# A four-layer network on one core: one lane of layer 1 at a time, an output product moved, and another start for the first head pair

## The chip, the core and the metric

The kernel runs on one core of one Trainium2 chip. The core has a matrix engine (PE, with its weight loads shown as PEld), a vector engine (DVE), a scalar engine (ACT), a general engine (POOL), and a sync engine (SP) that mostly issues transfers (DMA). They run side by side and wait for one another through semaphores. The metric is the device time of one execution in microseconds (us), lower is better. The kernel before takes 3713.06 us (median of 3 runs, 3712.05 to 3713.46).

## The reference

The input is `x`, 4 samples of 256 channels on a 48 x 48 grid (2304 positions), in float32. Four residual layers follow one another, each on the group-normalised `x`. Cut to what matters:

```python
x = x + L0(gn(x))   # 8 heads of 64: q, k, v = w_qkv @ x; q, k normalised over the positions;
                    # softmax(10 * q.k) over 2304 positions; times v; w_out
x = x + L1(gn(x))   # 3x3 max pool, blur to 16x16, depthwise taps along four directions,
                    # gate = sigmoid(sum), upsampled by 3; gn(x) * gate
x = x + L2(gn(x))   # one-head attention, softmax(theta.phi / 8), W, batch norm over all samples
x = x + L3(gn(x))   # channel gate, 3x3 depthwise convolution, instance norm, leaky relu

def _gn(v, G=32, eps=1e-5):
    g = v.reshape(B_, G, C_ // G, H_, W_)
    m, s = g.mean((2, 3, 4)), g.var((2, 3, 4))
    return (g - m) / sqrt(s + eps)
```

Layer 0 is by far the largest: 4 samples x 8 heads x 2304 x 2304 scores.

## The kernel before

Channels lie on 128 partitions in two halves (`k` = 0, 1). Layer 0 works sample by sample and head pair by head pair: 16 phases (4 samples `b` x 4 pairs `p`). A phase has 6 units of 384 query columns; a unit has 9 groups of 256 keys. Layer 2's attention follows with 12 more units, so there are 108. The main loop issues, for each group `t`, the scores of this group, the sums of the softmax denominators of the group before, work that is due in this place, and then the product with v of the group before. Beside it run "lanes": generators that issue a few instructions of other layers between the groups.

```python
for t, (u, g, st) in enumerate(groups):
    for j in range(g * G, (g + 1) * G):
        scores(u, j)                       # PE, then exp on ACT
    if prev is not None:
        add_up(*prev)                      # POOL (half), DVE (acc)
    do(due, t)
    ...
    do(fills, t)                           # jobs of this place, in the order of their rank
    clock["early"] = False
    lanes(st["others"], st, t + 0.5, ends) # other layers
    ...                                    # then weigh(pu, j): the product with v
    if pg == NG - 1:
        last(pu, t)                        # ACT copies av to raw; ends a unit
```

In the third group of a unit (`AT_CHUNK` = 2) stands the projection of the next pair, in the order of the ranks: q (1), v (2), then the output product of an earlier unit, half 0 (2.5), then k (3), then half 1 (4). All of them take turns in two PSUM tiles `pj`.

```python
def chunk(s):
    def end():
        qk(s, 1)
        squares(s)
        if s + 2 < NCH:
            fetch(s + 2)                   # 384 columns of x from memory into a tile xs
    return [(1, lambda: qk(s, 0)), (2, lambda: values(s)), (3, end)]

def out_proj(b, p, c, pair, o):
    ...
    return [((2.5, 4)[k], lambda k=k: part(k)) for k in range(NK)]
```

Layer 1 of sample b runs beside layer 0 of sample b + 1. For samples 0 to 2 it is one generator for both halves: statistics, maxima, blur, then 20 "rounds" of tap products (ACT) and sums (DVE), then the gate, its products with x (POOL) and additions (DVE). The places in a unit in which it may go on are given by `TURNS`, and by `ROUND` or `HASTE` for the rounds:

```python
TURNS, ROUND, HASTE = (2, 2, 3, 5, 6, 8), -1, -2
ROUND_TURNS = {ROUND: (2, 5, 8), HASTE: (2, 4, 6, 8)}
...
haste = HASTE if b == NX - 1 else ROUND    # NX = 3
...
for i, (b, p) in enumerate(order):
    ...
    if (b, p) == (2, 0):
        for s in range(NSL):
            work.setdefault(s + 2 * NG, []).append(lambda s=s: send(s))      # sample 0 to memory
            work.setdefault(s + 5 * NG, []).append(lambda s=s: receive(s))   # sample 3 in its place
    if b > 0:
        end = n - 2 if (b, p) == (B - 1, NPAIR - 1) else n + 1
        others.append((l1[b - 1], FREE, 2 if p == 0 else 0, end))
    if b > 1 and p == 0:
        others.append((l1[b - 2], FREE, 0, 4 * NG))
```

In the place `end - 1` of a phase a lane is run to its end at once, whatever is left of it. With `n + 1` this place never comes.

The start: x of sample 0 is loaded, group statistics are taken, and the first pair is projected from fetched tiles of x, chunk by chunk, before the attention begins:

```python
projs[0]["prefetch"]()                     # weights of pair 0
_drain(gn(0, norms0[0]))
projs[0]["norms"]()                        # weights times 1/deviation (ACT), bias for v
projs[0]["start"]()                        # fetches the first two tiles of x again
projs[1]["prefetch"]()
for s in range(NCH):
    for _, fn in projs[0]["chunk"](s):     # q, v, k, squares of q and k
        fn()
for fn in projs[0]["scale"]:               # 1/norms, q scaled
    fn()
projs[0]["out_bias"]()
projs[1]["norms"]()
for b in range(1, NX):
    load_x(b)                              # samples 1 and 2
attend(phases)
```

Of the kernel before, what the change touches and what calls it, by code (L numbers as in the profile page):

```python
# [14 lines left out]
P = 128  # L15
HW = 48
N = HW * HW
NK = 2
# [56 lines left out]
def usual_path(  # L75
# [27 lines left out]

    def load_x(b):
        for k in range(NK):
            nc.sync.dma_start(X[b][:, k, :], xv[:, k, b, :])

    load_x(0)
    vec = cpool.tile([P, 9, NK], F32, name="vec")
    nc.scalar.dma_start(vec, vecs)  # L110

# [34 lines left out]
    )  # L146
    ones = cpool.tile([P, D], F32, name="ones")
    nc.gpsimd.memset(ones, 1.0)
    mhalf = cpool.tile([P, NK], F32, name="mhalf")
    nc.gpsimd.memset(mhalf, -0.5)  # L150
    nb1 = cpool.tile([P, NK], F32, name="nb1")
    nc.vector.tensor_scalar(nb1, vec[:, V_B1, :], -1.0, None, ALU.mult)

# [10 lines left out]

    GN_TICKS = NSL + 4

    def gn(b, res, halves=range(NK), slices=range(NSL)):

        if "st" not in res:
            res["st"] = small.tile([P, NK, NSL, 6], F32, tag="gn_st", name="gn_st")  # L170
        st = res["st"]
        for s in slices:
            for k in halves:
                nc.vector.bn_stats(st[:, k, s, :], X[b][:, k, s * SL : (s + 1) * SL])
            if s % 2 or len(halves) == NK:
                yield 0
        mv = small.tile([P, NK, 2], F32, tag="gn_mv", name="gn_mv")
        for k in range(NK):
            nc.vector.bn_aggr(mv[:, k, :], st[:, k].rearrange("p s f -> p (s f)"))
        yield 3  # L180
        ps = pj_tile()
        nc.tensor.matmul(ps[:, 0:NK], lhsT=gmat, rhs=mv[:, :, 0], start=True, stop=True)
        gm = small.tile([P, NK], F32, tag="gn_gm", name="gn_gm")
        nc.vector.tensor_copy(gm, ps[:, 0:NK])
# [200 lines left out]
    def attend(phases):  # L385


        groups = []
        for units, work, others in phases:
            for slot, fns in work.items():  # L390
                fills.setdefault(len(groups) + slot, []).extend(fns)
            st = {"others": [[gen, n, a, z, 0, 0] for gen, n, a, z in others], "at": 0}
            groups += [(u, g, st) for u in units for g in range(NG)]
        prev = None

        def lanes(some, st, t, ends):
            for lane in some:
                gen, n, a, z, done, ready = lane
                until = -(-n * (st["at"] + 1 - a) // (z - a))
                clock["final"] = final = st["at"] == z - 1  # L400
                while final or (done < until and t >= ready and not ends):
                    wait = next(gen, None)
                    if wait is None:
                        break
                    done, ready = done + 1, t + wait
                lane[4:] = done, ready

        def do(table, t):

            jobs = [job if isinstance(job, tuple) else (5, job) for job in table.pop(t, ())]  # L410
            for _, fn in sorted(jobs, key=lambda job: job[0]):
                fn()

        for t, (u, g, st) in enumerate(groups):
            for j in range(g * G, (g + 1) * G):
                scores(u, j)
            if prev is not None:
                add_up(*prev)
            do(due, t)

            ends = prev is not None and prev[1] == NG - 1
            clock["t"], clock["slot"] = t, st["at"] % NG

            clock["early"] = True
            if clock["slot"] == AT_AFTER % NG:
                lanes([lane for lane in st["others"] if lane[1] == FREE], st, t, ends)
            do(fills, t)
            clock["early"] = False
            lanes(st["others"], st, t + 0.5, ends)
            st["at"] += 1  # L430
            if prev is not None:
                pu, pg = prev
                for j in range(pg * G, (pg + 1) * G):
                    weigh(pu, j)
                if pg == NG - 1:
                    last(pu, t)
            prev = (u, g)
        pu, pg = prev
        add_up(pu, pg)
        for j in range(pg * G, (pg + 1) * G):  # L440
            weigh(pu, j)
        last(pu, len(groups))
        for t in sorted(set(due) | set(fills)):
            do(fills, t)
            do(due, t)
# [3 lines left out]
    def project(b, norm, pair):  # L449

        p = pair["p"]
        xs = {}
        at = {}

# [28 lines left out]
        def start():  # L483
            pair["q"] = big.tile([P, N], F32, tag="q", name="q")
            pair["k"] = big.tile([P, N], F32, tag="k", name="k")
            pair["v"] = big.tile([P, JB, P], F32, tag="v", name="v")
            at["ss"] = small.tile([P, 2, NSL], F32, tag="ss", name="ss")
            at["bias"] = small.tile([P, 2], F32, tag="bias", name="bias")
            fetch(0)
            fetch(1)  # L490

        def out_bias():
            ps = pj_tile()
# [12 lines left out]
        def qk(s, t):  # L506
            cols = slice(s * SL, (s + 1) * SL)
            to = pair["qk"[t]][:, cols]
            n = SL + (s == 0)
            ps = pj_tile()  # L510
            for k in range(NK):
                nc.tensor.matmul(  # L512
                    ps[:, :n], lhsT=at["w"][:, k, t, :], rhs=xs[s][:, k, :n],
                    start=k == 0, stop=k == NK - 1,
                )
            if s == 0:
                nc.scalar.copy(at["bias"][:, t : t + 1], ps[:, SL:n])
            nc.scalar.activation(to, ps[:, :SL], AF.Identity, bias=at["bias"][:, t : t + 1])  # L518

        def squares(s):  # L520

# [38 lines left out]
        def rescale(c0, c1):  # L560
# [8 lines left out]

        return {  # L570
            "prefetch": prefetch, "norms": norms, "start": start, "out_bias": out_bias,
            "chunk": chunk,
            "scale": [
                scale, lambda: rescale(0, 1), lambda: rescale(1, 3), lambda: rescale(3, 6)
            ],
# [2 lines left out]
    def out_proj(b, p, c, pair, o):  # L578
# [11 lines left out]
                xs, ps[:, :SL], pair["bo"][:, k : k + 1], xs, ALU.add, ALU.add  # L590
            )

        return [((2.5, 4)[k], lambda k=k: part(k)) for k in range(NK)]

    def l0_unit(b, p, c, pair):
        hold = {}
# [68 lines left out]
    ]  # L665
    L1_BUF = (NT + 1) * AS * AS

    TURNS, ROUND, HASTE = (2, 2, 3, 5, 6, 8), -1, -2
    ROUND_TURNS = {ROUND: (2, 5, 8), HASTE: (2, 4, 6, 8)}

    def paced(gen):

        at, count, wait, turns = -9, 0, 0, TURNS
        while True:
# [9 lines left out]
            if wait is None:  # L684
                return
            at, count = t, count + 1
            turns = ROUND_TURNS.get(wait, TURNS)
            yield 0

    def maxima(b, k, res):  # L690
# [60 lines left out]

    def strips(b, k, norm, res):


        haste = HASTE if b == NX - 1 else ROUND
        pd = padded(k, norm, res)

        bufs = [
# [11 lines left out]
                )  # L770

        products(0)
        yield haste
        products(1)
        yield haste
        for n, taps in enumerate(ROUNDS):
            last = n == len(ROUNDS) - 1
            if n + 2 < len(ROUNDS):
# [5 lines left out]
            nc.vector.tensor_reduce(  # L784
                to, bufs[n % 3][:, :, : min(n, 1) + len(taps)], AX.X, ALU.add
            )
            yield haste

    TAPS_AT_ONCE = 12

# [370 lines left out]
    for i, (b, p) in enumerate(order):  # L1161
# [16 lines left out]
                work[NG * s + AT_CHUNK] = slices[s]  # L1178
        if (b, p) == (2, 0):
            for s in range(NSL):  # L1180
                work.setdefault(s + 2 * NG, []).append(lambda s=s: send(s))
                work.setdefault(s + 5 * NG, []).append(lambda s=s: receive(s))
        if (b, p) == (0, 0):
            others.append((tap_weights(), WEIGHT_TICKS, 2, n - 2))
        if b > 0:
            end = n - 2 if (b, p) == (B - 1, NPAIR - 1) else n + 1
            others.append((l1[b - 1], FREE, 2 if p == 0 else 0, end))
        if b > 1 and p == 0:
            others.append((l1[b - 2], FREE, 0, 4 * NG))
        if (b, p) == (B - 1, NPAIR - 1):  # L1190
            others.append((part(ahead, L1_AHEAD, False), L1_AHEAD, n - L1_AHEAD - 3, n))
        if p == 1 and b + 1 < B:
# [30 lines left out]
        phases.append(([l2_unit(b, c, twos[b]) for c in range(L2C)], work, others))  # L1223

    projs[0]["prefetch"]()
    _drain(gn(0, norms0[0]))
    projs[0]["norms"]()
    projs[0]["start"]()
    projs[1]["prefetch"]()
    for s in range(NCH):  # L1230
        for _, fn in projs[0]["chunk"](s):
            fn()
    for fn in projs[0]["scale"]:
        fn()
    projs[0]["out_bias"]()
    projs[1]["norms"]()
    for b in range(1, NX):
        load_x(b)
    attend(phases)
    for k in range(NK):  # L1240
        w_stats(B - 1, k, L2C - 1)
# [1214 lines left out]
```

## Time and profile before

| | before |
|---|---|
| median of the runs | 3713.06 us |
| span of the profiled run | 3710.8 us |
| mean granted clock of PE | 0.980 |
| first scores of layer 0 | 51.9 us |
| layer 0, all samples, beside layer 1 of samples 0 to 2 | 51.9 to 2992 us |
| layer 2's attention, beside layer 1 of sample 3 | 2992 to 3442.8 us |
| layer 3 | 3442.8 us to the end |
| DMA | 97.89 MB, mean 26 GB/s |

The costliest rows of the profile are these. The columns are: line, engine, operation, output and input tiles, shape, count; then busy time in us and the mean of one in ns; then the idle time of the engine just before them and what ended it.

```profile
L244 ACT ACTIVATE pt<-sc 128x768 f32<-128x768 f32 x1944 | 1476.5, 812 | 814.1 <-PE sc L238 805.4
L269 POOL TENSOR_TENSOR half<-pt 128x768 f32<-128x768 f32 x477 | 954.1, 2001 | 1673.4 <-ACT pt L244 1611.7
L238 PE MATMUL sc<-q,k 64*64 64x384 f32 x13824 | 1279.6, 485 | 12.7 <-ACT pt L244 9.9
L258 PE MATMUL av<-pt,v 64*64 64x384 f32 x13824 | 1279.8, 485 | 0.0
L284 DVE TENSOR_TENSOR acc<-acc,pt 128x768 f32<-128x768 f32 x792 | 930.7, 1175 | 86.2 <-DVE acc L284 1.8
```

PE waits for almost nothing before its two large groups of matmuls, while ACT and POOL wait much for PE and ACT. A busy PE in such a table means that instructions follow one another without a gap; a matmul's end is modelled, so start to start is the better measure of one.

### The profile page before, as it was taken

The numbers are of one execution on the slowest core, as the hardware profiler recorded it, in microseconds if no ns is written. First come the engines' busy times: TensorE is split into PE (matmuls) and PEld (weight loads), VectorE is DVE, ScalarE is ACT, GpSimd is POOL, SyncE is SP. The second block draws the span as 40 slices with busy tenths as digits, with TensorE's granted clock in tenths as the row PEclk, the third lists the DMA queues.
The fourth block names the chain that finished last, engine by engine and source line by source line (L and its number), as shares of the span: only waits on it lengthen the run. The fifth ranks groups of instructions, "written<-read, shape, count | busy, mean of one in ns | idle before, by whom it ended". The sixth has DMA issues, their size and how long they took to land.

```text
span 3710.8 us, 86538 instructions
## 1 busy us (share of the span) xinstructions
PE 3522.4 (95%) x36330; PEld 1759.4 (47%) x36330; DVE 2588.3 (70%) x3203; ACT 2344.5 (63%) x3819; POOL 1444.7 (39%) x900
## 2 busy tenths in 40 slices
PE   7999999999999999999999999999999998999685
PEld 4444444454444444444444444444444445654343
DVE  2455555476778777967787779767968786576687
ACT  4665666666776677557766775587578555555353
POOL 2333333333334333433343334433433455664242
PEclk9999999999999999999999999999999999999797
DMA  4111111111111111121111111111111100000001
GB/s 138 24 25 21 26 21 26 21 25 21 25 21 26 20 29 17 34 55 34 21 25 21 25 21 25 21 25 21 25 16 25 17 6 6 6 8 4 26 29 74
DMA packets 114591, 97.89 MB, mean 26 GB/s; under 512 B 56224, under 2 KB 111632, under 8 KB 112400
## 3 DMA queue, kind: packets, MB, share of 16 engines
q1 hardware_dynamic: 111728, 91.27, 12.8%
q8 instruction: 286, 4.69, 0.5%
q10 hardware_dynamic: 2464, 1.00, 0.1%
q14 instruction: 113, 0.93, 0.1%
HBM read 59.33 MB, written 11.80 MB: 19 GB/s over the span
## 4 chain that ended last, share of the span: by engine, by line
PE 68%; DVE 18%; issue 5%; ACT 4%; POOL 3%; DMA 2%; SPq 0%; DVEq 0%; ACTq 0%; POOLq 0%
PE av L258 26%; PE sc L238 26%; DVE acc L284 7%; PE pj L512 6%; PE pj L584 3%; PE pj L533 3%; DVE sc L1446 2%; PE pj L291 1%; POOL half L269 1%; ACT pt L244 1%; DVE av L1446 1%; DVE acc L278 1%; PE pj L828 1%; ACT prod L766 1%; DMA xs<-in_x_dram 1%
## 5 line engine op out<-in xcount | busy, mean ns | idle before, releaser
L244 ACT ACTIVATE pt<-sc 128x768 f32<-128x768 f32 x1944 | 1476.5, 812 | 814.1 <-PE sc L238 805.4
L269 POOL TENSOR_TENSOR half<-pt 128x768 f32<-128x768 f32 x477 | 954.1, 2001 | 1673.4 <-ACT pt L244 1611.7
L238 PE MATMUL sc<-q,k 64*64 64x384 f32 x13824 | 1279.6, 485 | 12.7 <-ACT pt L244 9.9
L258 PE MATMUL av<-pt,v 64*64 64x384 f32 x13824 | 1279.8, 485 | 0.0
L284 DVE TENSOR_TENSOR acc<-acc,pt 128x768 f32<-128x768 f32 x792 | 930.7, 1175 | 86.2 <-DVE acc L284 1.8
L238 PEld LDWEIGHTS sc<-q,k 64*64 64x64 f32 x13824 | 510.6, 133 | 638.2 <-issue 499.9
L258 PEld LDWEIGHTS av<-pt,v 64*64 64x64 f32 x13824 | 514.4, 133 | 594.0 <-issue 557.3
L284 DVE TENSOR_TENSOR acc<-acc,half 128x768 f32<-128x768 f32 x459 | 468.6, 1021 | 335.7 <-POOL half L269 334.1
L589 DVE SCALAR_TENSOR_TENSOR x<-pj,bo,x 128x384 f32<-128x384 f32 x192 | 118.0, 615 | 461.9 <-PE pj L584 461.7
L512 PE MATMUL pj<-xs,w 128*128 128x384 f32 (+1 forms) x768 | 298.5, 512 | 3.2 <-issue 1.7
L766 ACT ACTIVATE prod<-pd,wt 128x256 f32<-128x256 f32 x486 | 280.6, 743 | 0.2
L339 POOL TENSOR_TENSOR o<-o,rinv 128x384 f32<-128x384 f32 x95 | 128.9, 1356 | 284.3 <-DMA rinv<-rinv 273.2
L512 PEld LDWEIGHTS pj<-xs,w 128*128 128x128 f32 x768 | 131.0, 190 | 157.3 <-issue 53.9
L584 PE MATMUL pj<-o,wo 128*128 128x384 f32 x384 | 159.8, 501 | 33.3 <-DVE x L589 28.7
L258 PE MATMUL av<-pt,qv 64*64 64x384 f32 x1728 | 173.9, 496 | 0.0
L238 PE MATMUL sc<-qv,kd 64*64 64x384 f32 x1728 | 169.4, 486 | 2.4 <-ACT pt L244 2.4
L784 DVE TENSOR_REDUCE prod<-prod 128x256 f32<-128x1280 f32 x114 | 168.5, 1478 | 0.0
L278 DVE TENSOR_TENSOR acc<-pt 128x768 f32<-128x768 f32 x99 | 139.3, 1407 | 26.4 <-ACT pt L244 26.4
L533 PEld LDWEIGHTS pj<-w,xs 128*128 128x128 f32 x1152 | 143.8, 192 | 26.0 <-issue 0.6
L533 PE MATMUL pj<-w,xs 128*128 128x128 f32 x1152 | 144.1, 275 | 0.0
L518 ACT ACTIVATE k<-pj,bias 128x384 f32<-128x384 f32 x96 | 55.7, 580 | 127.5 <-PE pj L512 127.0
L335 POOL TENSOR_TENSOR o<-raw 128x384 f32<-128x384 f32 x95 | 117.7, 1238 | 0.0
(226 smaller groups left out, 2686.7 us busy)
## 6 DMA issues: line engine op xcount, KB each, us to landing
xs<-in_x_dram SPq DMA_DIRECT2D x96, 384.0 KB
rinv<-rinv SPq DMA_DIRECT2D x208, 94.5 KB
x<-in_x_dram SPq DMA_DIRECT2D x6, 1152.0 KB
out_dram<-x SPq DMA_DIRECT2D x6, 1152.0 KB
l<-row SPq DMA_DIRECT2D x416, 1.5 KB
w<-in_wqkv_dram SPq DMA_DIRECT2D x32, 192.0 KB
rinv<-ls SPq DMA_DIRECT2D x208, 1.5 KB
x_out<-x SPq DMA_DIRECT2D x6, 384.0 KB
```

The source lines that it names most:

```text
L238: nc.tensor.matmul(ps[c * D : (c + 1) * D, h, :SL], lhsT=u["of"]["k"][r, j0 : j0 + D], rhs=u["of"]["q"][r, u["qc"]], start=True, stop=True,)
L244: nc.scalar.activation(pt, ps[:, :, :SL], AF.Exp, scale=u["scale"])
L258: nc.tensor.matmul(u["av"][h * D : (h + 1) * D, half, :SL], lhsT=value(u, j, h)[r], rhs=pt[r, h, :], start=j == 0, stop=j == JB - 1,)
L269: nc.gpsimd.tensor_add(half, pts[0], pts[1])
L278: nc.vector.tensor_add(u["acc"], ready[0], ready[1])
L284: nc.vector.tensor_add(u["acc"], u["acc"], term)
L339: eng.tensor_mul(o, o, u["rinv"])
L512: nc.tensor.matmul(ps[:, :n], lhsT=at["w"][:, k, t, :], rhs=xs[s][:, k, :n], start=k == 0, stop=k == NK - 1,)
L533: nc.tensor.matmul(ps[:, i * P : (i + 1) * P], lhsT=xs[s][:, k, i * P : (i + 1) * P], rhs=at["w"][:, k, 2, :], start=k == 0, stop=k == NK - 1,
L584: nc.tensor.matmul(ps[:, :SL], lhsT=wo[:, p, k * P : (k + 1) * P], rhs=o["o"], start=True, stop=True,)
L766: nc.scalar.activation(bufs[n % 3][:, :, min(n, 1) + i].rearrange("p (r c) -> p r c", c=AS), pd[:, PAD + dr : PAD + dr + AS, PAD + dc : PA ...
L784: nc.vector.tensor_reduce(to, bufs[n % 3][:, :, : min(n, 1) + len(taps)], AX.X, ALU.add)
```

## The change

It has three parts. Layer 1 of a sample must end within the four pairs of the next sample, so that there is never more than one lane of it, and its rounds go at the quicker pace for all three samples; sample 0 is then complete when sample 2 begins, and its store and the load of sample 3 move to the front of that sample. In sample 0's phases the first half of the output product comes directly after the scores, ahead of the sums and of the projections, so that the two PSUM tiles are taken in another order. At the start, x of sample 0 comes in over two queues, the statistics are taken half by half, the ACT table is loaded ahead, and the first pair is projected from x itself with q and k of all chunks ahead of v; DVE empties the k tiles; x of samples 1 and 2 is loaded later.

```diff
     def load_x(b):
         for k in range(NK):
-            nc.sync.dma_start(X[b][:, k, :], xv[:, k, b, :])
+            eng = nc.scalar if b == 0 and k else nc.sync
+            eng.dma_start(X[b][:, k, :], xv[:, k, b, :])
...
+    warm = cpool.tile([P, 1], F32, name="warm")
+    nc.scalar.activation(warm, mhalf[:, 0:1], AF.Exp)
...
+        if first:                              # group statistics of sample 0
+            for k in halves:
+                for s in slices:
+                    nc.vector.bn_stats(st[:, k, s, :], X[b][:, k, s * SL : (s + 1) * SL])
...
             for j in range(g * G, (g + 1) * G):
                 scores(u, j)
+
+            do(fills, t, lambda rank: rank < 1)
             if prev is not None:
                 add_up(*prev)
...
+            if direct:                         # start() of the first pair
+                for s in range(NSL):
+                    xs[s] = X[b][:, :, s * SL : (s + 1) * SL]
+            else:
+                fetch(0)
+                fetch(1)
...
+            if s == 0 and direct:              # qk(): the mean as a column of its own
+                for k in range(NK):
+                    nc.tensor.matmul(
+                        ps[:, SL : SL + 1], lhsT=at["w"][:, k, t, :],
+                        rhs=norm["nm"][:, k : k + 1], start=k == 0, stop=k == NK - 1,
+                    )
             if s == 0:
-                nc.scalar.copy(at["bias"][:, t : t + 1], ps[:, SL:n])
-            nc.scalar.activation(to, ps[:, :SL], AF.Identity, bias=at["bias"][:, t : t + 1])
+                nc.scalar.copy(at["bias"][:, t : t + 1], ps[:, SL : SL + 1])
+            if direct and t:
+
+                nc.vector.tensor_scalar(to, ps[:, :SL], at["bias"][:, t : t + 1], None, ALU.add)
+            else:
+                nc.scalar.activation(to, ps[:, :SL], AF.Identity, bias=at["bias"][:, t : t + 1])
...
-        return [((2.5, 4)[k], lambda k=k: part(k)) for k in range(NK)]
+        return [((2.5 if b else 0, 4)[k], lambda k=k: part(k)) for k in range(NK)]
...
-    TURNS, ROUND, HASTE = (2, 2, 3, 5, 6, 8), -1, -2
-    ROUND_TURNS = {ROUND: (2, 5, 8), HASTE: (2, 4, 6, 8)}
+    TURNS, ROUND, ROUND_TURNS = (2, 2, 3, 5, 6, 8), -1, (2, 4, 6, 8)
...
         if (b, p) == (2, 0):
             for s in range(NSL):
-                work.setdefault(s + 2 * NG, []).append(lambda s=s: send(s))
-                work.setdefault(s + 5 * NG, []).append(lambda s=s: receive(s))
+                work.setdefault(s, []).append(lambda s=s: send(s))
+                work.setdefault(s + NG, []).append(lambda s=s: receive(s))
         if (b, p) == (0, 0):
+            for c in range(1, NX):
+                work.setdefault(10 * c, []).append(lambda c=c: load_x(c))
             others.append((tap_weights(), WEIGHT_TICKS, 2, n - 2))
         if b > 0:
-            end = n - 2 if (b, p) == (B - 1, NPAIR - 1) else n + 1
+            end = n - 2 if p == NPAIR - 1 else n + 1
             others.append((l1[b - 1], FREE, 2 if p == 0 else 0, end))
-        if b > 1 and p == 0:
-            others.append((l1[b - 2], FREE, 0, 4 * NG))
...
     for s in range(NCH):
-        for _, fn in projs[0]["chunk"](s):
-            fn()
+        for t in range(2):
+            projs[0]["qk"](s, t)
+        projs[0]["squares"](s)
     for fn in projs[0]["scale"]:
         fn()
+    for s in range(NCH):
+        projs[0]["values"](s)
     projs[0]["out_bias"]()
     projs[1]["norms"]()
-    for b in range(1, NX):
-        load_x(b)
     attend(phases)
```

The cuts are marked with "..."; remarks after # in the added lines are set here for the reader, and an indentation may differ from the kernel's.

More of the change, by code (lines that the diff above doesn't have):

```diff
@@ L105, in load_x @@
         for k in range(NK):
-            nc.sync.dma_start(X[b][:, k, :], xv[:, k, b, :])
+            eng = nc.scalar if b == 0 and k else nc.sync
+            eng.dma_start(X[b][:, k, :], xv[:, k, b, :])
     load_x(0)
+    mhalf = cpool.tile([P, NK], F32, name="mhalf")
+    nc.gpsimd.memset(mhalf, -0.5)
     vec = cpool.tile([P, 9, NK], F32, name="vec")
@@ L148, in usual_path @@
     nc.gpsimd.memset(ones, 1.0)
-    mhalf = cpool.tile([P, NK], F32, name="mhalf")
-    nc.gpsimd.memset(mhalf, -0.5)
+    warm = cpool.tile([P, 1], F32, name="warm")
+    nc.scalar.activation(warm, mhalf[:, 0:1], AF.Exp)
     nb1 = cpool.tile([P, NK], F32, name="nb1")
@@ L165, in usual_path, with gn @@
     GN_TICKS = NSL + 4
-    def gn(b, res, halves=range(NK), slices=range(NSL)):
+    def gn(b, res, halves=range(NK), slices=range(NSL), first=False):
         if "st" not in res:
@@ L171, in gn @@
         st = res["st"]
-        for s in slices:
+        if first:
+            for k in halves:
+                for s in slices:
+                    nc.vector.bn_stats(st[:, k, s, :], X[b][:, k, s * SL : (s + 1) * SL])
+        for s in () if first else slices:
             for k in halves:
@@ L406, in lanes, with do @@
                 lane[4:] = done, ready
-        def do(table, t):
+        def do(table, t, which=lambda rank: True):
             jobs = [job if isinstance(job, tuple) else (5, job) for job in table.pop(t, ())]
-            for _, fn in sorted(jobs, key=lambda job: job[0]):
+            table[t] = [job for job in jobs if not which(job[0])]
+            for _, fn in sorted((job for job in jobs if which(job[0])), key=lambda job: job[0]):
                 fn()
@@ L451, in project @@
         p = pair["p"]
+        direct = b == 0 and p == 0
         xs = {}
@@ L488, in start @@
             at["bias"] = small.tile([P, 2], F32, tag="bias", name="bias")
-            fetch(0)
-            fetch(1)
+            if direct:
[4 more added lines that the diff above has]
+                fetch(1)
         def out_bias():
@@ L508, in qk @@
             to = pair["qk"[t]][:, cols]
-            n = SL + (s == 0)
+            n = SL + (s == 0 and not direct)
             ps = pj_tile()
@@ L571, in project @@
             "prefetch": prefetch, "norms": norms, "start": start, "out_bias": out_bias,
-            "chunk": chunk,
+            "chunk": chunk, "qk": qk, "squares": squares, "values": values,
             "scale": [
@@ L686, in paced @@
             at, count = t, count + 1
-            turns = ROUND_TURNS.get(wait, TURNS)
+            turns = ROUND_TURNS if wait == ROUND else TURNS
             yield 0
@@ L752, in strips @@
     def strips(b, k, norm, res):
-        haste = HASTE if b == NX - 1 else ROUND
         pd = padded(k, norm, res)
@@ L772, in strips @@
         products(0)
-        yield haste
+        yield ROUND
         products(1)
-        yield haste
+        yield ROUND
         for n, taps in enumerate(ROUNDS):
@@ L786, in strips @@
             )
-            yield haste
+            yield ROUND
     TAPS_AT_ONCE = 12
@@ L1225, in usual_path @@
     projs[0]["prefetch"]()
-    _drain(gn(0, norms0[0]))
+    _drain(gn(0, norms0[0], first=True))
     projs[0]["norms"]()
```

## The prediction

> **What bounds the kernel now.** I read the page first (busy shares, then the chain of work that ended last):
>
> ```profile
> PE 3522.4 (95%) x36330; PEld 1759.4 (47%) x36330; DVE 2588.3 (70%) x3203; ACT 2344.5 (63%) x3819; POOL 1444.7 (39%) x900
> ...
> PE 68%; DVE 18%; issue 5%; ACT 4%; POOL 3%; DMA 2%; SPq 0%; DVEq 0%; ACTq 0%; POOLq 0%
> ```
>
> PE sets the end wherever it is fed; 18% of the chain runs through DVE, and that part is worth asking for. To find where, I cut the span into stages. Each attention unit (one head pair, 384 query columns, nine groups) ends with the ACT copy of `av` to `raw`; the 108 starts of that copy give the edges of units 0 to 107. Busy times by stage (length; then PE, PEld, DVE, ACT, POOL; granted clock, DMA share, GB/s), for the start and the attention of samples 0, 1, 2 and 3:
>
> ```profile
> 0.00:51.90 51.90, 28.50 (x136) 20.88 (x136) 8.43 (x30) 19.71 (x49) 3.36 (x15) 1.00 0.59 199
> 51.90:768.50 716.60, 716.29 (x7720) 356.21 (x7724) 369.51 (x507) 433.60 (x688) 244.35 (x183) 1.00 0.14 26
> 768.50:1501.00 732.50, 725.65 (x7724) 349.94 (x7720) 549.42 (x642) 514.39 (x854) 274.30 (x158) 1.00 0.13 23
> 1501.00:2248.40 747.40, 730.03 (x7728) 350.86 (x7724) 571.07 (x668) 514.96 (x854) 285.75 (x163) 0.99 0.16 29
> 2248.40:2992.00 743.60, 721.64 (x7708) 346.39 (x7704) 573.44 (x673) 511.60 (x834) 288.34 (x166) 0.99 0.13 22
> ```
>
> Sample 0 has no layer 1 beside it: 716.6 us, PE busy in all of them. That is the floor, 29.6 us for a usual unit, about 30.3 where the matmuls for the biases of the next pair are added. Sample 1 pays 15.9 us above it for layer 1 of sample 0. Samples 2 and 3 pay 14.9 and 11.1 us more than sample 1. Unit by unit, this extra lies in one place, the second and third unit of the sample. The second unit of sample 1, then the second and third of sample 2, then the second of sample 3:
>
> ```profile
> 798.10:828.30 30.20, 30.17 (x328) 15.19 (x324) 25.49 (x32) 17.82 (x28) 9.85 (x6) 1.00 0.12 20
> ...
> 1531.30:1571.10 39.80, 32.36 (x328) 15.48 (x324) 36.93 (x44) 18.07 (x29) 17.34 (x9) 0.91 0.11 21
> 1571.10:1606.00 34.90, 32.87 (x332) 15.57 (x328) 25.88 (x42) 17.78 (x29) 13.48 (x9) 0.95 0.36 92
> ...
> 2278.80:2318.50 39.70, 32.26 (x328) 15.48 (x324) 36.87 (x43) 18.02 (x28) 17.23 (x8) 0.91 0.10 15
> ```
>
> In the slow units DVE is busy for 36.9 of 39.8 us, with 44 instructions for 32. The waits of 1531 to 1571 us say what this does:
>
> ```profile
> POOL half L269 <- DVE acc L284: 12.4, 1, 12.4
> PEld pj L584 <- DVE x L589: 7.2, 1, 7.2
> PE pj L584 <- DVE x L589: 6.6, 1, 6.6
> ```
>
> PE stands 6.6 us because the output projection's PSUM tile has not been emptied: the DVE add (L589) is queued behind maxima of the new lane, gate additions (L892) of the old lane, and sums that run 2.2 to 2.4 us each instead of 0.95.
>
> At the start, the chain and the timeline show two loads one behind the other, a table load, and a tail before the first scores:
>
> ```profile
> 0.81 5.27 DMA x<-in_x_dram
> 6.10 5.07 DMA x<-in_x_dram
> ```
>
> ```profile
> 20.84 1.28 ACT L479 ACT_TABLE_LOAD   x1 [20.84 <-PE pj L472]
> ...
> 51.42 1.68 DVE L568 TENSOR_SCALAR q<-q,qsc 128x384 f32<-128x384 f32 x3
> 51.90 0.21 PEld L238 LDWEIGHTS sc<-q,k 64*64 64x64 f32 x8 [2.46 <-DVE q L568]
> ```
>
> [...] the same DVE sum takes 0.95 us alone and 2.4 us around the POOL gate products (2.31 us each). So layer 1 work next to attention costs more than its own time. [...] The 39.8 us unit shows 0.91 granted clock; a stall is paid a second time. [...] Here the second half's DMA is issued at 6.10 us, after the first has landed at 6.08, and DMA moves only 69 GB/s in the microsecond from 6 to 7 against 437 at 4 to 5; so here two queues should be worth that gap, not double bandwidth. [...]
>
> **The change, part by part.**
>
> *One lane at a time.* Samples 0 and 1's layer 1 now advance four rounds a unit instead of three, and must end inside the next sample; the overlap of two lanes in the first four units of samples 2 and 3 goes. Units 48, 49, 50 took 30.4 + 39.7 + 34.9 = 105.0 us and units 72, 73, 74 took 30.4 + 39.7 + 32.5 = 102.6. Without an older lane they have what units 24, 25, 26 have, 29.6 + 30.3 + 30.6 = 90.5. Gains 14.5 and 12.1, together 26.6 us.
>
> The faster pace is already seen: sample 2's layer 1 uses it. Its 13 units from 2413.3 to 2811.8 us take 398.5; the same 13 positions in sample 1 at three rounds (921.1 to 1319.2) take 398.1. A round unit costs some 0.6 us either way and there are fewer of them. In sample 3 the last gate falls in units 92 and 93, 28.9 us each, that stage's floor, and the lane is done by unit 94, so the forced finish at the end of the fourth pair should find nothing. I allow 1 us over samples 1 and 2 for the gate that moves in.
>
> *Storing and reloading* move from slots 18 and 45 of sample 2's first pair to 0 and 9, the same places inside a unit. POOL waited 7.1 us for `rinv` as the stores began, and unit 50 was 2.4 us longer than unit 74, which has no stores. Part of this may follow the stores to unit 48: +1 us (estimate).
>
> *The start.* x is 2.36 MB; at 430 GB/s (an estimate from the 424 to 437 of full microseconds) both halves need 5.5 us after a start at about 2, so by 8; `vec`, now behind x in its queue and needed by DVE before its statistics, perhaps by 9. The 12 statistics (5.6 us) then end near 14.5 instead of 16.3: -1.9. The table load taken ahead: -1.3. PE starts near 19.7 instead of 22.85. From there to the first scores it was 29.05 us. Now q and k: 12 x 1.29 = 15.5, the two mean columns 0.3, v: 6 x 1.34 = 8.0, output bias and next pair's biases 1.3, waits 0.5: 25.6. Squares, rsqrt and the scaling of q (3.6 us) run beside the v matmuls; k emptied by DVE leaves ACT 0.6 + 1.3 = 1.9 us a chunk against PE's 2.6. So -3.4. Sum: -6.6 us. Loads of samples 1 and 2 in slots 10 and 20 (5 us each at that rate) may delay a `rinv` in sample 0, where DVE has half its time free: 0.
>
> *Output product first, sample 0.* In the timeline of sample 0:
>
> ```profile
> 477.00 0.48 ACT L538 COPY v<-pj 128x384 f32<-128x384 f32 x1 [0.76 <-PE pj L533]
> 477.53 0.94 PEld L512 LDWEIGHTS pj<-xs,w 128*128 128x128 f32 x4 [0.54 <-ACT v L538]
> ```
>
> The k weights wait 0.54 us for v's PSUM tile, but PE works on the output product meanwhile: the four k matmuls take 1.40 us start to start, against 1.29 for four such matmuls in a row. The new order of the two PSUM tiles removes that wait, so 0.1 us, at most 22 times: 2; I take -1.5.
>
> Sum: -26.6 + 1 + 1 - 6.6 - 1.5 = -32.7, and 3713.06 - 32.7 = 3680. Layers 2 and 3 (from 2992 us on) are untouched.
>
> **Rivals.** *DVE work moved, not removed:* gate, additions and statistics of the second half stall PE in the last units of samples 1 and 2. For: sample 2's first-half gate unit has DVE busy 31 us. Against: sample 3 does it at floor, though with lighter projections there. It would leave some 15 of 26 us: 3691. *ACT becomes the bound:* at four rounds ACT instruction times sum to 31.8 us a unit (overlapping), above the 29.6; samples 1 and 2 also carry group statistics in the second pair. If 1 us more per round unit, 20 units: 3700. Against: 30.3 us in sample 3. *The wait of the k weights is all on the path:* 22 x 0.5 = 11 us: 3670. Against: the start-to-start times. *The start gains little,* because both queues share the engines and `vec` comes last: only 3 us: 3684. *Forced finish:* a lane not done in time would be run out at one place, over 20 us lost. Its schedule counts groups, as in sample 3, so I doubt it.
>
> **Range and chances.** The 26.6 rests on three measured units and may miss by 5; the start by 2.5; the rest by 3. So 3680, 8 in 10 between 3670 and 3692. Faster by 2% needs 3639, more than twice the stall I find: 0.01. Slower by 2% needs a new stall of over 100 us: 0.02.
>
> **What would show it.** First scores near 45 us; samples 1, 2, 3 of 732 to 733, 733 to 735 and 731 us; sample 0 at 715; units 49 and 73 near 30.3 with DVE under 28 busy and no wait of L584 on L589; clock 1.00 there. It is wrong if units 44 to 47 or 68 to 71 grow by more than 1 us each, if one unit near the end of a sample is over 40 us, or if the first scores stay after 49 us.

## The result and the profile after

The changed kernel takes 3684.73 us (median of 4 runs, 3680.2 to 3689.91) against 3712.56 us before. The ratio is 0.9925, with a 95% interval of 0.9908 to 0.9943. The prediction said 3680, between 3670 and 3692. The profiled run has a span of 3685.0 us, 25.8 less than before. First the same two lines of its page, busy shares and chain:

```profile
PE 3516.1 (95%) x36338; PEld 1766.9 (48%) x36338; DVE 2520.1 (68%) x3209; ACT 2343.6 (64%) x3814; POOL 1423.6 (39%) x899
...
PE 71%; DVE 14%; issue 6%; ACT 5%; POOL 4%; DMA 1%; SPq 0%; DVEq 0%; ACTq 0%; POOLq 0%
```

The part of the chain that runs through DVE has fallen from 18% to 14%. The same stages as before (start; attention of samples 0, 1, 2, 3; then layer 2's attention), with the length of each in the second column:

```profile
0.00:47.48 47.48, 29.62 (x145) 22.22 (x145) 13.40 (x38) 16.41 (x43) 3.25 (x14) 1.00 0.33 104
47.48:758.60 711.12, 710.65 (x7721) 357.56 (x7724) 369.17 (x504) 434.35 (x690) 243.76 (x181) 1.00 0.16 30
758.60:1497.50 738.90, 729.11 (x7728) 350.94 (x7724) 541.12 (x668) 515.82 (x855) 277.04 (x164) 1.00 0.14 24
1497.50:2236.90 739.40, 727.83 (x7728) 350.56 (x7724) 537.97 (x668) 515.74 (x854) 275.43 (x165) 1.00 0.16 29
2236.90:2967.90 731.00, 719.70 (x7700) 346.90 (x7696) 542.42 (x647) 510.83 (x832) 275.54 (x161) 1.00 0.14 21
2967.90:3416.60 448.70, 414.48 (x4688) 244.64 (x4680) 311.89 (x362) 238.68 (x382) 264.40 (x147) 0.97 0.06 6
```

| stage | before | after | difference | foreseen |
|---|---|---|---|---|
| to the first scores | 51.9 | 47.5 | -4.4 | -6.6 |
| sample 0 | 716.6 | 711.1 | -5.5 | -1.5 |
| sample 1 | 732.5 | 738.9 | +6.4 | about +0.5 |
| sample 2 | 747.4 | 739.4 | -8.0 | -13 |
| sample 3 | 743.6 | 731.0 | -12.6 | -12.1 |
| layer 2's attention | 450.8 | 448.7 | -2.1 | 0 |
| layer 3 | 268.0 | 268.4 | +0.4 | 0 |

The slow units are gone: units 49 and 73, 39.8 and 39.7 us before, are the second and third line here. The first line is unit 35, which took 30.1 us before.

```profile
1094.20:1130.60 36.40, 33.48 (x328) 15.99 (x324) 29.92 (x39) 19.07 (x31) 15.52 (x11) 0.91 0.15 28
1527.10:1557.40 30.30, 30.27 (x328) 15.20 (x324) 24.17 (x32) 17.87 (x29) 10.46 (x6) 1.00 0.37 98
2266.50:2296.80 30.30, 30.27 (x328) 15.19 (x324) 25.60 (x32) 17.84 (x29) 9.90 (x6) 1.00 0.12 20
```

Units 49 and 73 have DVE busy for 24.2 and 25.6 us instead of 36.9, and PE without a gap. Unit 35 has taken over their look: a granted clock of 0.91 and a gap. Unit 59, its equal in sample 2, takes 34.9 us (30.1 before). So the large stall was removed and a smaller one came in. Over the whole kernel PE's waits for the emptying of the output product tell the same; the first line is of the kernel before, the second of the changed one (us in total, times, longest):

```profile
PE pj L584 <- DVE x L589: 28.7, 16, 6.6
```

```profile
PE pj L610 <- DVE x L615: 17.9, 11, 2.9
```

### The profile page after: what moved, and what is told of

Read it like the earlier page. It is cut to its first block, busy times and chain, and to the rows that moved or that the text cites. A ratio compares the mean times of both kernels' runs of the same rounds, so it can differ in the third digit from the quotient of the medians.

```text
span 3685.0 us, 86525 instructions
## 1 busy us (share of the span) xinstructions
PE 3516.1 (95%) x36338; PEld 1766.9 (48%) x36338; DVE 2520.1 (68%) x3209; ACT 2343.6 (64%) x3814; POOL 1423.6 (39%) x899
## 4 chain that ended last, share of the span: by engine, by line
PE 71%; DVE 14%; issue 6%; ACT 5%; POOL 4%; DMA 1%; SPq 0%; DVEq 0%; ACTq 0%; POOLq 0%
PE sc L246 27%; PE av L266 27%; PE pj L528 6%; DVE acc L292 5%; PE pj L610 3%; PE pj L559 3%; POOL half L277 2%; DVE sc L1471 2%; ACT pt L252 2%; PE pj L299 1%; ACT prod L789 1%; DVE av L1471 1%; PE pj L851 1%; DVE acc L286 1%; PE pj L967 1%
## 5 line engine op out<-in xcount | busy, mean ns | idle before, releaser
L277 POOL TENSOR_TENSOR half<-pt 128x768 f32<-128x768 f32 x477 | 939.9, 1972 | 1729.0 <-ACT pt L252 1650.1
L292 DVE TENSOR_TENSOR acc<-acc,pt 128x768 f32<-128x768 f32 x792 | 885.2, 1118 | 84.4 <-DVE acc L292 2.3
L292 DVE TENSOR_TENSOR acc<-acc,half 128x768 f32<-128x768 f32 x459 | 473.6, 1032 | 349.2 <-POOL half L277 348.3
L615 DVE SCALAR_TENSOR_TENSOR x<-pj,bo,x 128x384 f32<-128x384 f32 x192 | 118.2, 616 | 512.3 <-PE pj L610 512.0
L528 PE MATMUL pj<-xs,w 128*128 128x384 f32 (+1 forms) x720 | 275.4, 505 | 0.0
L610 PE MATMUL pj<-o,wo 128*128 128x384 f32 x384 | 160.7, 503 | 22.1 <-DVE x L615 17.9
L559 PEld LDWEIGHTS pj<-w,xs 128*128 128x128 f32 x1080 | 134.5, 191 | 24.1
L286 DVE TENSOR_TENSOR acc<-pt 128x768 f32<-128x768 f32 x99 | 131.7, 1331 | 12.5 <-ACT pt L252 12.5
L559 PE MATMUL pj<-w,xs 128*128 128x128 f32 x1080 | 134.9, 275 | 0.0
```

The lines of the kernel that those rows point to most:

```text
L277: nc.gpsimd.tensor_add(half, pts[0], pts[1])
L286: nc.vector.tensor_add(u["acc"], ready[0], ready[1])
L292: nc.vector.tensor_add(u["acc"], u["acc"], term)
L528: nc.tensor.matmul(ps[:, :n], lhsT=at["w"][:, k, t, :], rhs=xs[s][:, k, :n], start=k == 0, stop=k == NK - 1,)
L559: nc.tensor.matmul(ps[:, i * P : (i + 1) * P], lhsT=xs[s][:, k, i * P : (i + 1) * P], rhs=at["w"][:, k, 2, :], start=k == 0, stop=k == NK - 1,
L610: nc.tensor.matmul(ps[:, :SL], lhsT=wo[:, p, k * P : (k + 1) * P], rhs=o["o"], start=True, stop=True,)
```

## The experiments

### The parts one by one

**The pace alone**, in the kernel before:

```diff
-    ROUND_TURNS = {ROUND: (2, 5, 8), HASTE: (2, 4, 6, 8)}
+    ROUND_TURNS = {ROUND: (2, 4, 6, 8), HASTE: (2, 4, 6, 8)}
```

> The kernel before with one edit: layer 1 of samples 0 and 1 goes four rounds a unit instead of three. Theory (the pace ends the older lane in time, the rule of one lane only states it): units 48 to 50 and 72 to 74 fall from 105.0 and 102.6 us to about 91 each, and the gate of the first half, now in units 34 and 35 and 58 and 59, stalls PE there for 5 to 6 us each: 3695 to 3700 us. Rival (the rule in the list of lanes or the moved stores do it): units 49 and 73 stay at 39.7 us, 3712 us.

It takes 3692.07 us (ratio 0.9948, 0.9935 to 0.9962), 20.5 us less than the kernel before and 3 us less than the theory's range. Units 49 and 50, in the view of busy times:

```profile
1537.50:1567.80 30.30, 30.27 (x328) 15.20 (x324) 25.80 (x32) 17.87 (x29) 11.42 (x6) 1.00 0.15 26
1567.80:1598.30 30.50, 30.50 (x328) 15.07 (x324) 19.54 (x32) 17.80 (x28) 12.21 (x8) 1.00 0.41 104
```

Both are at the length of sample 1's, although nothing in the list of lanes was changed. The pace takes the overlap away. Unit 50 still has the stores of sample 0 in it (104 GB/s) and loses nothing to them. Units 35, 37, 38 and 59 take 34.8, 33.8, 31.6 and 34.9 us: the new stall comes with the pace too.

**The rule alone**, in the changed kernel: three rounds a unit again for samples 0 and 1, but a lane must still end in its sample.

```diff
-    TURNS, ROUND, ROUND_TURNS = (2, 2, 3, 5, 6, 8), -1, (2, 4, 6, 8)
+    TURNS, ROUND, HASTE = (2, 2, 3, 5, 6, 8), -1, -2
+    ROUND_TURNS = {ROUND: (2, 5, 8), HASTE: (2, 4, 6, 8)}
...
+        haste = HASTE if b == NX - 1 else ROUND     # and "yield haste" in strips()
```

> The changed kernel with the old pace of three rounds a unit for layer 1 of samples 0 and 1, but still with the rule that a lane ends in its sample. Theory (the pace is what makes room; the rule alone runs the rest of the lane out at one place): units 35 and 59 fall to 30.1, but units 47 and 71 grow by 8 to 15 us each; in all 3688 to 3700 us, about as slow as the changed kernel or slower. Rival (the rule alone is enough, whatever the pace): units 47 and 71 under 33 us and a time near 3672 us.

It takes 3722.93 us (ratio 1.0032, 1.0019 to 1.0044), slower than the kernel before. Units 47 and 71 take 52.7 and 53.4 us instead of 30.1; I had expected 8 to 15 us more, and it is 23. Unit 47, busy times and then PE's wait:

```profile
1460.80:1513.60 52.80, 33.26 (x332) 16.04 (x328) 36.84 (x54) 21.30 (x37) 19.01 (x13) 0.81 0.14 35
```

```profile
PE pj L190 <- DVE gn_mv L187: 18.7, 1, 18.7
```

The rest of the lane (gate, additions, statistics of the second half) stands in DVE's queue in one piece, and PE, which has a small matmul of these statistics in its own queue, waits 18.7 us for it. Units 35 and 59 are back at 30.1 us here, so the gate's new place and the stall go together.

**The start alone**, in the kernel before:

> The kernel before with the new start alone (two queues, table ahead, projection from x, q and k before v, later loads of samples 1 and 2). Theory: first scores at 47.5 us instead of 51.9 and the first unit 1.3 us shorter because PE comes to it without a pause: 5 to 6 us, 3707 us. Rival (transfers of samples 1 and 2, now beside the attention, take it back in the first pair): 3710 us or more, with a unit of the first pair over 30.3 us.

3704.76 us (ratio 0.9981, 0.9973 to 0.9989), 7.8 us less. The first scores come at 48.6 us (on this chip at 53.2 and 53.4 in two kernels with the old start), and no unit of the first pair is over 30.3 us: the late loads cost nothing.

**The output product first in sample 0, alone**, in the kernel before:

```diff
-        return [((2.5, 4)[k], lambda k=k: part(k)) for k in range(NK)]
+        return [((2.5 if b else 0, 4)[k], lambda k=k: part(k)) for k in range(NK)]
...
+            do(fills, t, lambda rank: rank < 1)      # after scores(), ahead of add_up()
```

> The kernel before with the output product first in sample 0 alone. Theory (both the q and the k matmuls then have their weights loaded ahead, 1.29 us instead of 1.40 for each four): 0.22 us for each of some 22 units, 4 to 5 us, 3708 us; units of sample 0 at 29.4 us. Rival (the prediction's: k alone): 2 us, 3711 us.

3709.77 us (ratio 0.999, 0.9984 to 0.9997), 2.8 us less; units 2 to 25 are 0.2 us shorter each, 29.4 instead of 29.6 for a usual one. In the trace that makes some 5 us for the 24 units, as the theory had it; the runs alone (1.1 to 5.9 us less) do not tell it from the rival's 2. The three parts alone give 20.5 + 7.8 + 2.8 = 31.1 us, all together 27.8. In the profiles, units 35 and 37 together take the same in the changed kernel (36.4 + 32.1 us) as with the pace alone (34.8 + 33.8), and unit 69 takes 32.7 instead of 30.6; the rest of the 3.3 us is within the spread of the runs.

### What makes unit 35 long

The gate of the first half used to fall in units 36 and 37 and now falls in units 34 and 35. The timeline of the changed kernel, DVE, POOL and PE in unit 35:

```profile
1099.43 3.84 DVE L292 TENSOR_TENSOR acc<-acc,pt 128x768 f32<-128x768 f32 x2
1100.14 2.31 POOL L913 TENSOR_TENSOR x<-x,gate 128x768 f32<-128x768 f32 x1
...
1104.33 0.95 DVE L915 TENSOR_TENSOR x<-x,l1acc 128x768 f32<-128x768 f32 x1
1105.19 0.61 DVE L615 SCALAR_TENSOR_TENSOR x<-pj,bo,x 128x384 f32<-128x384 f32 x1
...
1105.86 1.65 PE L610 MATMUL pj<-o,wo 128*128 128x384 f32 x2 [2.92 <-DVE x L615]
...
1108.08 2.84 PE L266 MATMUL av<-pt,v 64*64 64x384 f32 x16
```

The sums L292 that run beside the POOL gate product take 1.9 us each instead of 1.0, one gate addition stands directly ahead of the emptying L615, and PE waits 2.92 us. Then the two matmuls L610 take 1.65 us instead of 0.81, and the av group behind them, at 1108.08, has its successor only 2.6 us later instead of 1.29. The granted clock (the third number from the end of each line) over these stretches:

```profile
1105.80:1108.00 2.20, 2.14 (x6) 1.54 (x6) 0.46 (x2) 0.24 (x1) 0.00 (x0) 0.50 0.03 7
1108.00:1113.00 5.00, 5.00 (x37) 2.09 (x41) 4.21 (x8) 1.62 (x3) 0.00 (x0) 0.55 0.00 0
1113.00:1118.00 5.00, 5.00 (x68) 2.19 (x64) 1.92 (x3) 3.15 (x6) 2.46 (x2) 1.00 0.03 1
```

For 7 us PE ran at half clock. I estimate the work lost at half of that, about 3.4 us, more than the wait itself: 2.9 + 3.4 = 6.3, and unit 35 grew by 6.2. To see whether the place of the gate is the cause, I let its products and additions begin only in the fourth group of a unit, behind the projections, in the changed kernel:

```diff
         up2 = acc.unsqueeze(3).to_broadcast([P, AS, AS, 3])
+        while b < NX and clock["slot"] != 3 and not clock["final"]:
+            yield 1
         for i in range(4):
```

> The changed kernel, but the gate's products and additions of samples 0 to 2 wait for the fourth group of a unit, behind the projections. Theory (units 35, 59 and 69 stall because these DVE additions and the POOL products stand ahead of the emptying of the output product's PSUM tile): these units fall from 36.4, 34.9 and 32.7 us to about 30.5 each, and the time by 8 to 14 us against the changed kernel, to 3671 to 3677 us, with a smaller spread between its runs. Rival (DVE has too much work there whatever its order): the stall moves to the next unit and the time stays at 3680 to 3690 us.

It takes 3674.0 us (3671.43 to 3677.09; ratio 0.9897, 0.9882 to 0.9912). Units 35, 59 and 69 take 30.3, 30.3 and 29.6 us, and samples 1 and 2 take 733.1 and 733.8, close to the 732 to 733 and 733 to 735 of the prediction. Unit 35 here, and unit 36, in which the gate's statistics now fall:

```profile
1094.60:1124.80 30.20, 30.17 (x328) 15.20 (x324) 24.01 (x29) 18.83 (x30) 15.03 (x9) 1.00 0.11 15
1124.80:1156.30 31.50, 29.96 (x324) 14.59 (x320) 28.81 (x34) 18.16 (x30) 14.12 (x8) 1.00 0.19 39
```

The same work, some groups later, costs PE no wait in unit 35 and about 1.5 us in unit 36. Over the whole kernel PE waits for L615 fall to this:

```profile
PE pj L610 <- DVE x L615: 11.5, 12, 1.6
```

No single wait of this kind is over 1.6 us any more. So the rival, too much DVE work whatever its order, falls. The hold moves the POOL products and the DVE additions together; which of the two weighs how much is not shown. Since 10 us could come from another chip, both kernels ran once more on one chip.

> The changed kernel unedited, on the same chip as the next, for a direct comparison. Theory: 3680 to 3690 us, with units 35 and 59 at 34 to 37 us. Rival (the 10 us between this kernel and the one with the held gate came from the chips): the same time as the next.

> The kernel with the held gate again. Theory: 3671 to 3677 us, 8 to 13 us below the changed kernel on this chip, units 35, 59 and 69 at 30.5 us or less. Rival: 3680 us or more.

The changed kernel took 3686.22 us (3683.13 to 3688.14), the one with the held gate 3675.6 us (3672.56 to 3676.16; ratio to the kernel before 0.9896, 0.9881 to 0.9911). Every one of its runs is below every one of the other's; the means differ by 10.7 us. This version beats both kernels.

Unit 69, which has the gate of the second half, shows the same without a hold. Seven profiles have the quick pace, no hold, and the output product in its usual place in samples 1 to 3. Unit 69 takes 32.7 to 32.9 us in four of them and 30.6 in three. PE's wait in the changed kernel, and then in the kernel with one queue (below):

```profile
2154.95 0.91 PE L610 MATMUL pj<-o,wo 128*128 128x384 f32 x2 [2.77 <-DVE x L615]
```

```profile
2153.30 0.91 PE L610 MATMUL pj<-o,wo 128*128 128x384 f32 x2 [0.69 <-DVE x L615]
```

In the four long ones the gate's second addition starts 10.0 to 10.3 us into the unit, directly ahead of the emptying; in the three short ones it starts at 6.5 us. The three are those that load x of sample 0 over one queue; no run shows whether that is the reason.

### The output product first everywhere

```diff
-        return [((2.5 if b else 0, 4)[k], lambda k=k: part(k)) for k in range(NK)]
+        return [((0, 4)[k], lambda k=k: part(k)) for k in range(NK)]
```

> The changed kernel with the output product first in every sample, not in sample 0 alone. Theory (the 0.22 us a unit is had wherever DVE is not behind, and lost where it is: v's matmuls then need the PSUM tile that DVE must empty 2.7 us sooner): units of samples 1 to 3 with the gate or the maxima beside them get longer by 1 to 5 us each, the round units shorter by 0.2; on balance 0 to 10 us slower than the changed kernel, 3685 to 3695 us. Rival (DVE always comes in time, since the product's emptying stands ahead of the sums): 0.22 us for each of some 65 units, 14 us faster, near 3671 us.

It takes 3713.77 us (ratio 1.0003, 0.9995 to 1.0012), 29 us above the changed kernel, far more than the theory's 0 to 10. The direction was right, the size three times too small. PE waits for the same emptying, now at v's matmuls, over samples 1 to 3:

```profile
PE pj L559 <- DVE x L615: 44.0, 20, 4.9
```

There are 20 such waits, up to 4.9 us, in place of 11 up to 2.9. What follows a wait can be slow as well: in unit 42 v's twelve matmuls take 2.6 us after a wait of 2.35, instead of 1.34. The round units without a wait are 0.2 us shorter, as in sample 0. So the order is right where DVE is idle and wrong where it is late.

### The start

What stands between the loads and the first scores in the changed kernel, from its timeline:

```profile
8.96 1.02 DVE L179 BATCH_NORM_STATS2 gn_st<-x 128x6 f32<-128x384 f32 x2 [7.99 <-DMA x<-in_x_dram]
...
9.96 4.69 DVE L179 BATCH_NORM_STATS2 gn_st<-x 128x6 f32<-128x384 f32 x10
...
14.56 0.47 DVE L187 BATCH_NORM_AGGREGATE gn_mv<-gn_st 128x2 f32<-128x36 f32 x2
...
19.77 2.93 PE L528 MATMUL pj<-x,w 128*128 128x384 f32 x4 [0.34 <-ACT w L491]
...
22.49 0.85 PE L534 MATMUL pj<-gn_nm,w 128*128 128x1 f32 x4
...
47.48 1.52 PE L246 MATMUL sc<-q,k 64*64 64x384 f32 x16
```

The table load now stands at 15.9 us, beside the statistics' last steps, and off this path.

**One queue.** Both halves of x on the sync queue again (`eng = nc.sync`), the rest as changed.

> The changed kernel, with both halves of sample 0 on the sync queue again. Theory (the second half's transfer is issued only when the first has landed, which leaves the DMA engines empty between them): the statistics end near 16.3 us instead of 14.6 and first scores come 1.5 to 2 us later, at about 49.3 us; 3686 us. Rival (the shared DMA engines make it the same): first scores at 47.5 us.

```profile
6.92 2.85 DVE L179 BATCH_NORM_STATS2 gn_st<-x 128x6 f32<-128x384 f32 x6
...
11.90 2.86 DVE L179 BATCH_NORM_STATS2 gn_st<-x 128x6 f32<-128x384 f32 x6 [2.13 <-DMA x<-in_x_dram]
...
14.68 0.47 DVE L187 BATCH_NORM_AGGREGATE gn_mv<-gn_st 128x2 f32<-128x36 f32 x2
```

First scores at 48.0 us, 0.5 us later than with two queues, and 3683.4 us (ratio 0.9919, 0.9904 to 0.9934): no loss in the runs. My theory fell, though the rival's reason does not hold either: the rate is the same (while x of sample 0 comes in, the fullest microsecond moves 433 GB/s with two queues, and 437 with one in the kernel before), but the transfers are not. With one queue the first half lands at 6.9 us and its six statistics are done before the second lands at 11.9; with two both land at 9.0 and twelve statistics follow. Both ways the aggregation behind them starts at 14.6 to 14.7 us. To separate the two, the statistics went back to slices over both halves, once with one queue and once with two.

> The changed kernel with both halves of sample 0 on the sync queue and the statistics slice by slice over both halves, as before. Theory (the order by halves was enough, because the first half's six statistics then run while the second half lands): statistics end near 16.3 us and first scores near 49.3 us. Rival (something else of the new start brought the statistics forward): first scores at 47.5 to 48 us.

> The changed kernel with two queues, but the statistics slice by slice over both halves. Theory (either of the two is enough alone): statistics end near 14.7 us, first scores at 47.5 to 48 us. Rival (only the order counts): first scores near 49.3 us.

With one queue the aggregation starts at 16.35 us and the first scores come at 49.1; with two queues at 14.82 and 47.8 (one run each, 3687.8 and 3683.03 us). Either is enough alone; together they give hardly more than one.

**v between q and k**, as before, in the changed kernel:

```diff
-        for t in range(2):
-            projs[0]["qk"](s, t)
-        projs[0]["squares"](s)
+        projs[0]["qk"](s, 0)
+        projs[0]["values"](s)
+        projs[0]["qk"](s, 1)
+        projs[0]["squares"](s)
```

> The changed kernel, with v of each chunk between q and k at the start, as before. Theory (the squares, the norms and the scaling of q then stand behind the last matmul): first scores 2.5 to 3.5 us later, at 50 to 51 us, and the first unit 31 us instead of 29.7 because PE comes to it after a pause; 3688 to 3690 us. Rival (ACT is what binds the start in either order): first scores within 1 us of 47.5.

3686.72 us (ratio 0.9929, 0.9914 to 0.9944), not told apart from the changed kernel by the runs; the traces do it. First scores at 50.65 us, 3.2 later, and a first unit of 32.0 us:

```profile
50.17 1.68 DVE L594 TENSOR_SCALAR q<-q,qsc 128x384 f32<-128x384 f32 x3
50.65 0.31 PEld L246 LDWEIGHTS sc<-q,k 64*64 64x64 f32 x8 [2.02 <-DVE q L594]
```

PE waits 2 us for the scaling of q, and the granted clock is 0.50 from 50.65 to 56 us. In the changed kernel PE comes to the scores out of v's matmuls and the first unit takes 29.7 us.

## Why the prediction was right, and where its steps were off

The total was right, 3680 against 3684.73, and for a good part by the reason given; three sizes were off, one of them by a wrong step. That the total came so near is in part luck: samples 1 and 2 gave 10.9 us less than foreseen and the start 2.2 less, while samples 0 and 3 and layer 2 gave 6.6 us more.

**One lane at a time: right.** "Units 48, 49, 50 took 105.0 us and units 72, 73, 74 took 102.6 ... Without an older lane they have 90.5." They took 29.6 + 30.3 + 30.6 = 90.5, both times. The experiments add what I had not seen: the pace does this, and the kernel with the rule but the old pace is 10 us slower than the kernel before, for all that the start and the output product give.

**"I allow 1 us over samples 1 and 2 for the gate that moves in": the step that failed.** I read the quick pace from sample 3, where the same gate fell in unit 83 and cost 0.9 us, and took it for samples 1 and 2. There the gate's first two additions on DVE came about 3.6 us, roughly one group, later (0.9 and 10.1 us into unit 35; 2.7 us before unit 83 and 6.5 us into it in the same trace). The second then stood directly ahead of the emptying, and unit 35 cost 6.2 us, unit 59 4.7 and unit 69 2.5 in that run. PE's three waits were equal (2.9, 2.9 and 2.8 us); the half clock behind them was not (last section). That accounts for what samples 1 and 2 have above the foreseen lengths (about 6 us each). The held gate shows the place of the gate to be the cause. Why it comes later than in sample 3 is open; the statistics of the next sample's first normalisation run beside it in samples 1 and 2 only, but no run took them away. Of my rivals, "DVE work moved, not removed" was right in kind; it named the second half's gate in the last units of the sample, which came true in unit 69 alone, and not in every profile; units 35 and 59 have the first half's, in the middle. The prediction read from unit 49 of the kernel before that a stall is paid a second time: PE's wait of 6.58 us ends at 1547.77 us there, and the granted clock is 0.50 until 1551.59. In unit 35 it was paid twice too: 2.9 us of wait, then 0.50 until 1112.53 us. In unit 69 it was not: the wait of 2.77 us was followed by 1.00. I had counted the second payment for the stall that goes and not for one that comes.

**ACT at four rounds a unit: the rival fell.** Round units take 30.2 to 31.2 us, as in sample 3 before.

**Stores and loads moved: +1 foreseen, 0 measured.** Unit 48 takes 29.6 us with the stores in it, and unit 50 took 30.5 with them when only the pace was changed. The 2.4 us in which unit 50 exceeded unit 74 in the kernel before came only with the overlap.

**The start: -6.6 foreseen, -4.4 to the first scores and another -1.3 in the first unit.** PE's start was foreseen at 19.7 us and was 19.77. From there I had 25.6 us and it was 27.7. Of the 2.1 missing, 1.4 lie in the first four matmuls, which take 2.72 us (19.77 to 22.49) instead of 1.29; the four for the mean column behind them take 0.7. I took the later duration for all. The kernel before had the same slow first matmuls, but they were inside its measured 29.05. The profile's clock column shows 1.00 there, but the trace holds no record of the clock before 23.68 us (25.83 in the kernel before). From that record on, matmuls of this shape follow one another every 0.32 us instead of every 0.64, so my estimate from this spacing is half clock before it. The 1.3 us in the first unit is half clock too: in the kernel before, PE paused 2.37 us ahead of the scores and then had 0.50 from 53.14 to 56.55 us. I had counted the pause but not what came after it. This part need not come in every execution: with the pace alone, the same pause of 2.37 us was followed by 1.00 and a first unit of 29.7 us, as in the changed kernel; with the output product alone it was followed by 0.50 until 59.27 us, and the first unit took 32.0. By the runs, the start alone gave 7.8 us (4.1 to 10.0). My reason for -1.9 of it, two queues, was only half the matter: either of two changes gives it.

**The output product: -1.5 foreseen, some -4 in the trace.** The timeline of sample 0 in the changed kernel:

```profile
466.81 1.45 PE L528 MATMUL pj<-xs,w 128*128 128x384 f32 x4
468.10 1.50 PE L559 MATMUL pj<-w,xs 128*128 128x128 f32 x12
469.43 1.46 PE L528 MATMUL pj<-xs,w 128*128 128x384 f32 x4
470.73 0.81 PE L610 MATMUL pj<-o,wo 128*128 128x384 f32 x2
```

Both groups of four take 1.29 to 1.30 us start to start; before, both took 1.40. I counted k's, which waited for a PSUM tile, and not q's, which came first after the 64 x 64 matmuls; that place now belongs to the output product, at no added cost (0.75 us against 0.73). So it is 0.2 us a unit, of which I had foreseen half.

**Layer 2, -2.1 us, belongs to no part.** It lies in units 97 and 98 (34.1 + 43.1 us); a second profile of the same kernel has 32.5 + 47.2, as the kernel before.

## What to carry to other kernels

When a background task is moved or sped up, look at what stands in the queue of the shared engine ahead of the one operation that the bound engine waits for: here the same additions cost 6 us in one place and under 2 some groups later. Read the cost of a new place from a stretch that has the same neighbours, not only the same task, and do not count a gap on PE at its own length alone (here waits of 2.8 to 2.9 us cost 2.5, 4.7 and 6.2 us). A limit that forces a task to its end is only safe when the task has been given the pace to be done by then.

## What the runs showed that I had not expected

How unequal the half clock behind equal gaps is. In layer 0 of the changed kernel the granted clock falls to 0.50 three times: at 1105.70 us for 6.83 us (unit 35), at 1846.39 for 3.41 (unit 59) and at 2795.30 for 6.83. Here is what follows the waits of 2.92, 2.94 and 2.77 us in units 35, 59 and 69; the clock is the third number from the end:

```profile
1105.70:1112.53 6.83, 6.67 (x34) 3.38 (x38) 4.77 (x9) 1.39 (x3) 0.00 (x0) 0.50 0.01 2
1846.39:1849.80 3.41, 3.41 (x25) 1.51 (x28) 3.20 (x6) 0.97 (x2) 0.00 (x0) 0.50 0.00 0
1849.80:1853.21 3.41, 3.41 (x47) 1.55 (x44) 1.10 (x3) 2.27 (x4) 1.35 (x1) 1.00 0.02 5
2154.95:2161.78 6.83, 6.83 (x78) 3.23 (x82) 4.27 (x5) 2.79 (x5) 2.16 (x1) 1.00 0.02 3
```

So the length of the gap does not settle the cost: three waits within 0.2 us of one another are followed by 6.83 us, by 3.41 us and by nothing at 0.50. What decides is not shown. If half of that time is lost, an estimate, the wait and the loss are 2.9 + 3.4 = 6.3 us for unit 35, 2.9 + 1.7 = 4.6 for unit 59 and 2.8 for unit 69, against 6.2, 4.7 and 2.5 measured. In the kernel before, the same gate costs 0.9 us in unit 83, where the wait is 1.0 us and the clock behind it 1.00, and here it costs 6 in unit 35.

Besides, a forced finish of one lane cost 23 us, of which 18.7 are one wait of PE for a matmul on two columns.
